# A graph stack on one core: the third hop's weights folded into the first hop's, its sums turned by VectorE or by TensorE

## Chip, cores and metric

The kernel runs on one core of a Trainium2 chip. The time is device microseconds of one execution; the median of three runs before the change is 708.03 us (707.58 to 708.05). One more execution was recorded by the hardware profiler, and all lines quoted are from that one.

The engines carry their names as the profile writes them: PE is TensorE (PEld its weight loads), DVE VectorE, ACT ScalarE, POOL GpSimd, SP SyncE, which issues the loads of the adjacency.

## What is computed

A stack of four small graph networks over one graph of 3327 nodes with 64 features, all in fp32, each with a layer norm and a relu ahead of it and a residual around it. The change concerns the third, whose weight matrix is the adjacency squared element by element (`left_weights` and `A` are both `adj`):

```python
def _L2_gnn_ref(x, A, left_weights, W0, b0, W1, b1, W2, b2):
    w = left_weights * A
    for W, b in ((W0, b0), (W1, b1), (W2, b2)):
        x = w @ x
        x = x @ W.T + b
    return x
...
    # --- layer 2 (adj_preln) ---
    h = jnp.maximum(_layernorm(x, axis=-1), 0.0)
    x = x + _L2_gnn_ref(h, adj, adj, L2_gnn_W0, L2_gnn_b0, L2_gnn_W1, L2_gnn_b1, L2_gnn_W2, L2_gnn_b2)
```

No function that isn't linear stands between the three hops, so a weight on the right of one hop can be applied on the right of an earlier one. A bias that is added before a hop has to pass that hop too.

## The kernel before

**Tiles.** The 3327 nodes are padded to 26 blocks of 128, in two halves of 13. A tile of the adjacency holds 128 source nodes (its partitions) against the destination nodes of a group, for both halves. The 13 destination blocks of a half form four chunks, 0 to 3, of 384, 384, 384 and 512 columns; chunks 0 and 1 are group 0, chunks 2 and 3 group 1. One unit of work (`propagate`, L579) multiplies one tile into the sums of one chunk: two matmuls, one for each half, into the upper and lower 64 partitions of a PSUM bank, so that the sums come out as features by nodes (64 features of each half on 128 partitions). The sources of the next hop are wanted as nodes by features, so each hop's sums are turned around once.

**Hops.** There are eight, k = 0 to 7. 0 and 1 belong to a gated cell, 2 is a ranked sum, 3 to 5 are the three hops of the third network, with squared adjacency, and 6 and 7 belong to the last one. `after_k` (L938 to L1021) is what happens to a chunk whose sums of hop k are complete; `y[k+1]` holds its result for the next hop.

**Order.** The adjacency is read from HBM again and again, since the 20 slots (`slots`, L120) hold less than half of it. `joint(g, k, sweep, later, keep)` (L655) lets a tile serve two hops while it is there: hop k for both chunks of a group, and hop k + 1 of the same group `later` tiles afterwards. So joint(1, 4) runs hops 4 and 5 of group 1, then joint(0, 5) runs hops 5 and 6 of group 0, then joint(1, 6). The first tiles of joint(0, 5) are those whose sources lie in group 1: hop 6 wants `y[6]` of chunk 2 first, after `later` + 1 tiles of hop 5.

All this is written into a list of units at build time; `run` (L711) walks through it and issues the instructions of each engine in that order. What `after_k` does is a generator that yields an estimated number of microseconds; `spend` (L374) counts them down as units pass, so the steps of such a task are strewn among the units. Each engine then runs its own list strictly as written, with semaphores between engines.

**Squares.** A unit of hops 3 to 5 needs its tile squared. In joint(1, 2), (0, 3) and (1, 4) that is done in place once for each chunk; in joint(0, 5) the squares go into other rooms, halves of a slot (`Mask`, L419), since hop 6 wants the plain tile. Squares are issued some units ahead (`expand`, L484, up to 3; `prepare`, L444, up to 6). Who does them is decided at build time, by whether any task of a chunk is open:

```python
    def square(sq, v, turn):
        if turn % 3 or any(ch in tasks or (2, ch) in sums for ch in range(NC)):
            nc.scalar.activation(sq, v, AF.Square)
        else:
            nc.vector.tensor_tensor(sq, v, v, ALU.mult)
```

**PSUM.** There are eight banks, four named `sum` and four named `temp`; `take` and `give` (L316, L329) pass them around by age.

**Weights of the third network.** `bd` (L123) holds four block-diagonal 128x128 matrices: 0 the weight of the second network, 1 to 3 W0, W1 and W2, transposed. `brow` has the biases b0, b1, b2 spread over all partitions, `hopcol` has columns of biases. `product(i, j)` (L205) replaces `bd[i]` by `bd[i]` times `bd[j]`: a pair of matmuls turns `bd[i]`, ScalarE copies, a second pair multiplies, ScalarE copies back. `fold_hops` (L219), which runs once, around 223 to 231 us, multiplies W0 by W1 in this way and passes b0 through W1. Then:

- after_3 (L973) copies the sums, multiplies by `bd[1]` on TensorE, which also turns them, and adds `brow[0]`.
- after_4 (L985) has no weight left to apply: `sums_to_nodes` (L807) copies the sums on ScalarE with the bias column b1 and lets VectorE turn them, in 16 transposes of 32x32 blocks for a chunk.
- after_5 (L988) copies the sums (VectorE for even chunks, ScalarE for odd ones), multiplies by `bd[3]`, W2, on TensorE (`dense_to_nodes`, L759), adds the result from PSUM to x (`residual`, L852), normalizes for hop 6, and at the end turns `y[6]` to features on VectorE (`transpose_on_vector`, L796), which after_6 reads much later.
- b2 is added to x long before, at the end of after_2 (L961), 15 estimated microseconds after the rest of that task, by `add_row` (L859).

Of the kernel before, what the change touches and what calls it, by code (L numbers as in the profile page):

```python
# [9 lines left out]
F32 = mybir.dt.float32  # L10
BF16 = mybir.dt.bfloat16
I16 = mybir.dt.int16
AF = mybir.ActivationFunctionType
ALU = mybir.AluOpType
# [30 lines left out]
N, D = 3327, 64  # L45
P = 128
# [8 lines left out]
CWM = 512  # L55
GROUPS = [(0, 1), (2, 3)]
# [9 lines left out]
WL1, WL2, WL3 = 14, 15, 18  # L66
# [21 lines left out]
def sources_of(*chunks):  # L88
    return [s * NB + b for c in chunks for s in range(2) for b in range(*CH[c])]


def upper(n):
    return slice(n * D, (n + 1) * D)
# [3 lines left out]
def kernel(  # L97
# [9 lines left out]
    nc = tc.nc  # L107
# [3 lines left out]
    work = ctx.enter_context(tc.tile_pool(name="work", bufs=4))  # L111
# [11 lines left out]
    bd = const.tile([P, 4, P], F32, name="bd")  # L123
# [8 lines left out]
    hopcol = const.tile([P, 2], F32, name="hopcol")  # L132
    ident = const.tile([P, P], F32, name="ident")
# [71 lines left out]
    def product(i, j):  # L205

        n, ps = take()
        mm(ps[:, :P], bd[:, i, :], ident)
        tr = work.tile([P, P], F32, name="t2")
        nc.scalar.copy(tr, ps[:, :P])  # L210
        give(n)
        yield 1.0
        n, ps = take()
        mm(ps[:, :P], tr, bd[:, j, :])
        nc.scalar.copy(bd[:, i, :], ps[:, :P])
        give(n)
        yield 1.0

    def fold_hops():  # L219

        i, ps = take()
        for n in range(3):
            for h in range(2):
                nc.tensor.matmul(ps[upper(h), n * P:(n + 1) * P], brow[:, n], ident, start=True, stop=True)
        cols = work.tile([P, CWM], F32, name="t2")
        nc.scalar.copy(cols[:, :3 * P], ps[:, :3 * P])
        give(i)
        yield 1.0

        i, ps = take()  # L230
        mm(ps[:, :D], cols[:, :P], bd[:, 2, :D])
        nc.vector.tensor_copy(brow[:, 0], ps[:, :D])
        nc.vector.tensor_copy(hopcol[:, 0:1], cols[:, P:P + 1])
        give(i)
        yield 1.0
        yield from product(1, 2)
# [59 lines left out]
    def blocks(c):  # L296
        return CH[c][1] - CH[c][0]

    def width(c):
        return blocks(c) * P  # L300

    def mm(out, lhsT, rhs, start=True, stop=True):


        for h in range(2):
            hs = slice(h * D, (h + 1) * D)
            nc.tensor.matmul(out[hs], lhsT[:, hs], rhs, start=start, stop=stop)  # L307
# [8 lines left out]
    def take(sums=False, either=True):  # L316


        either = either and not sums
        pool = idle_sums if sums else idle_temps  # L320
        if either and idle_sums and (not pool or released[idle_sums[0]] < released[pool[0]]):
            pool = idle_sums
        for c in list(tasks):
            if not pool and c not in running:
                advance(c)
        i = pool.popleft()
        return i, banks[i]

    def give(i):  # L329
        released[i] = max(released) + 1  # L330
        (idle_sums if i < 4 else idle_temps).append(i)

    def nodes(c):

        return feat.tile([P, blocks(c), 2, D], F32, name=f"y{c}")

    def flat(t):
        return t.rearrange("p b s d -> p b (s d)")
# [4 lines left out]
    def xchunk(c):  # L343
        return xs[:, CH[c][0]:CH[c][1]]

    def view(ps, c):
        return ps[:, :width(c)].rearrange("p (b f) -> p b f", f=P)
# [5 lines left out]
    def advance(c):  # L353
        running.add(c)
        try:
            tasks[c][1] = next(tasks[c][0])
        except StopIteration:
            del tasks[c]
        running.discard(c)
# [257 lines left out]
    def put(k, c, t):  # L617
        units.append((k, c, t))
        if k == COUNT or KIND[k] != RANKED or c == GROUPS[t.g][0]:
            t.uses += 1  # L620
# [34 lines left out]
    def joint(g, k, sweep, later, keep, lag=None):  # L655


        a, b = GROUPS[g]
        in_place = KIND[k] != PLAIN and KIND[k + 1] == SQUARED
        early = (KIND[k], KIND[k + 1]) == (PLAIN, RANKED)  # L660
        waiting = deque()
        counting = Counting(g, lag)

        def both(t):
            for c in (a, b):
                put(k, c, t)
            if lag is not None:
                counting.add(t)

        def second(n):  # L670
            for _ in range(n):
                if waiting:
                    t = waiting.popleft()
                    for c in (a, b):
                        put(k + 1, c, t)

        for q in sources_of(*GROUPS[1 - g]):
            t = Tile(q, g, in_place, early)
            both(t)
            waiting.append(t)  # L680
            if len(waiting) > later:
                second(1)
        own = [[Tile(q, g, in_place, early) for q in sources_of(c)] for c in (a, b)]
        all_own = own[0] + own[1]
        for n, t in enumerate(all_own[:-sweep]):
            both(t)
            second(len(waiting) + n + 1 > later if early else min(2, len(waiting) - keep))
        counting.rest()
        for c in (a, b):
            for t in all_own[-sweep:]:  # L690
                put(k, c, t)
                if lag is not None and c == a:
                    counting.add(t)
            if KIND[k] == RANKED:
                units.append((k, c, SPECIAL))
        counting.rest()
        second(len(waiting))
        for t in own[0]:
            for c in (a, b):
                put(k + 1, c, t)  # L700
        for c in (a, b):
            for t in own[1]:
                put(k + 1, c, t)
            if KIND[k + 1] == RANKED:
                units.append((k + 1, c, SPECIAL))
# [44 lines left out]
    def evacuate(acc, c, busy=False):  # L750
        m = work.tile([P, CWM], F32, name="t2")[:, :width(c)]
        if c % 2 or busy:
            nc.scalar.copy(m, acc[0][1][:, :width(c)])
        else:
            nc.vector.tensor_copy(m, acc[0][1][:, :width(c)])  # L755
        give(acc[0][0])
        return m

    def dense_to_nodes(ft, w, c):  # L759

        i, ps = take()
        v = view(ps, c)
        for b in range(blocks(c)):
            mm(v[:, b, :], ft[:, b * P:(b + 1) * P], bd[:, w - WL1, :])
        return i, v
# [41 lines left out]
    def sums_to_nodes(acc, c, bias):  # L807

        m = work.tile([P, CWM], F32, name="t2")[:, :width(c)]
        nc.scalar.activation(m, acc[0][1][:, :width(c)], AF.Identity, bias=hopcol[:, bias:bias + 1])  # L810
        give(acc[0][0])
        yield 0.8
        v = m.rearrange("p (b q n) -> p b q n", q=4, n=32)
        yk = nodes(c)
        for s in range(2):
            for f in range(2):
                at = s * D + f * 32
                for q in range(4):
                    nc.vector.transpose(yk[q * 32:(q + 1) * 32, :, s, f * 32:(f + 1) * 32], v[at:at + 32, :, q])  # L819
                yield 1.2  # L820
        return yk
# [30 lines left out]
    def residual(v, c, relu=False):  # L852
        if relu:
            nc.vector.scalar_tensor_tensor(flat(xchunk(c)), v[1], 0.0, flat(xchunk(c)), op0=ALU.max, op1=ALU.add)
        else:
            nc.vector.tensor_tensor(flat(xchunk(c)), flat(xchunk(c)), v[1], ALU.add)
        give(v[0])

    def add_row(c, i):  # L859

        n = 2 * blocks(c)
        nc.vector.tensor_tensor(groups(xchunk(c)), groups(xchunk(c)),
                                brow[:, i:i + 1, :].to_broadcast([P, n, D]), ALU.add)
# [97 lines left out]
    def after_2(c, acc):  # L961
        m = evacuate(acc, c)
        yield 1.4
        v = dense_to_nodes(m, WL1, c)
        yield 1.2
        residual(v, c)
        yk = nodes(c)
        yield from layernorm_relu(yk, c, squares_on_scalar=c in GROUPS[0])
        y[3][c] = yk
        yield 15.0  # L970
        add_row(c, 2)

    def after_3(c, acc):  # L973
        m = evacuate(acc, c)
# [11 lines left out]
        y[5][c] = yield from sums_to_nodes(acc, c, 0)  # L986

    def after_5(c, acc):  # L988
        m = evacuate(acc, c)
        yield 0.8  # L990
        v = dense_to_nodes(m, WL2 + 2, c)
        yield 0.8
        residual(v, c)
        yk = nodes(c)
        yield from layernorm_relu(yk, c)
        y[6][c] = yk
        yield 8.0
        yield from transpose_on_vector(yk, c)
# [30 lines left out]
    joint(1, 2, sweep=6, later=6, keep=1)  # L1029
    joint(0, 3, sweep=8, later=4, keep=4)  # L1030
    joint(1, 4, sweep=8, later=4, keep=4)
    joint(0, 5, sweep=8, later=4, keep=4)
    joint(1, 6, sweep=8, later=4, keep=4)
    alone(0, 7, sweep=6, parts=True)

# [50 lines left out]
```

## Time and profile before

| what | value |
|---|---|
| median of three runs | 708.03 us |
| profiled execution, its time | 707.41 us |
| profiled execution, its span | 705.5 us |
| mean granted TensorE clock | 0.999 |
| TensorE busy | 680.6 us |
| VectorE, ScalarE busy | 351.7, 271.3 us |
| third network's hops 3 to 5 | within some 285 to 561 us |
| matmuls of the units in fp32 (L607) | 3016 records, 533.6 us |
| end of hop 5 for group 1, group 0 | near 512, near 560 us |

The span runs from the first to the last instruction. A matmul in fp32 leaves two records, so a unit is four records of L607. A line of the timeline gives the start, the length, the engine, the line of the kernel, what was written from what, the shape, how many instructions were merged, and in brackets how long the engine had been idle and what released it. In the chain of waits each line is a start, a length, an engine and what ran.

### The profile page before, as it was taken

What the parts mean: (1) busy time and instruction counts of PE and PEld (TensorE: products, weight loads), DVE (VectorE), ACT (ScalarE), POOL (GpSimd) and SP (SyncE); (2) the same over time, 40 slices, a digit from 0 to 9 for tenths busy, and PEclk for the clock granted to TensorE, in tenths of its full rate; (3) what the DMA queues carried; (4) which work ended last, traced back from release to release, by engine and by line L of the source; (5) the groups of instructions that cost most, each with busy time, mean ns of one, the idle gap of its engine ahead of it and who ended that gap; (6) DMA issues with size and microseconds to landing.
All of it is one profiled execution on the core that took longest, in us unless ns stands there. A gap on an engine that the chain in (4) does not pass through costs nothing.

```text
span 705.5 us, 12624 instructions
## 1 busy us (share of the span) xinstructions
PE 680.6 (96%) x5100; PEld 362.5 (51%) x5100; DVE 351.7 (50%) x747; ACT 271.3 (38%) x421; POOL 75.7 (11%) x114
## 2 busy tenths in 40 slices
PE   1999999999999999999999999999999999999997
PEld 1454666643545787677444444333344444344464
DVE  7566835633997889847533105425271565005101
ACT  1014100212136888888997206832166500000101
POOL 4300000002291233111100000000000000000000
PEclk9999999999999999999999999999999999999999
DMA  9999996089688952683799649963997399917991
GB/s 337 401 387 404 405 406 239 1 337 384 204 284 299 313 176 83 241 296 103 266 369 354 242 163 408 405 262 112 392 366 271 105 397 405 407 64 282 403 402 36
DMA packets 68549, 201.31 MB, mean 285 GB/s; under 512 B 7228, under 2 KB 8228, under 8 KB 68492
## 3 DMA queue, kind: packets, MB, share of 16 engines
q1 hardware_dynamic: 65596, 199.46, 76.1%
q8 instruction: 40, 0.66, 0.4%
q10 hardware_dynamic: 720, 0.85, 0.3%
q0 software_dynamic: 2176, 0.20, 0.2%
q14 instruction: 17, 0.14, 0.1%
HBM read 199.45 MB, written 0.85 MB: 284 GB/s over the span
## 4 chain that ended last, share of the span: by engine, by line
PE 84%; DVE 9%; ACT 4%; issue 1%; DMA 1%; SPq 0%; ACTq 0%; DVEq 0%
PE sum L607 70%; PE temp L307 5%; ACT adj L440 4%; DVE adj L466 3%; PE temp L542 2%; PE temp L876 2%; PE sum L307 1%; PE temp L774 1%; PE sum L876 1%; DVE e L521 1%; DMA bd<-in_weights 1%; DVE both L825 1%; DVE adj L901 1%; DVE st L842 0%; DVE t L836 0%
## 5 line engine op out<-in xcount | busy, mean ns | idle before, releaser
L607 PE MATMUL sum<-adj,y 128*64 128x384 f32 (+3 forms) x3016 | 533.6, 501 | 0.8 <-DVE y L849 0.6
L607 PEld LDWEIGHTS sum<-adj,y 128*64 128x64 f32 x3016 | 233.7, 137 | 246.3 <-issue 220.9
L440 ACT ACTIVATE adj<-adj 128x768 f32<-128x768 f32 (+1 forms) x175 | 143.6, 892 | 47.3 <-PE sum L607 24.6
L466 DVE TENSOR_SCALAR adj<-adj 128x768 bf16<-128x768 f32 (+3 forms) x208 | 114.7, 599 | 39.1 <-PE temp L542 31.1
L824 ACT COPY both<-sum 64x384 f32<-64x384 f32 (+3 forms) x17 | 8.1, 478 | 196.4 <-PE sum L607 196.3
L607 PE MATMUL sum<-e,both 128*64 128x384 bf16 (+1 forms) x624 | 78.4, 339 | 0.5 <-DVE e L521 0.4
L523 ACT ACTIVATE e<-temp,bitsb 128x384 int16<-128x384 f32 (+1 forms) x117 | 66.1, 606 | 15.0 <-PE temp L307 9.9
L825 DVE COPY both<-sum 64x384 f32<-64x384 f32 (+3 forms) x17 | 9.7, 568 | 113.6 <-ACT both L824 112.4
L442 DVE TENSOR_TENSOR adj<-adj 128x768 f32<-128x768 f32 (+1 forms) x33 | 31.5, 1003 | 52.2 <-DMA adj<-in_adjT 33.4
L307 PE MATMUL temp<-adj,tri 128*64 128x384 bf16 (+1 forms) x332 | 56.8, 341 | 0.5 <-DVE e L521 0.2
L845 POOL TENSOR_TENSOR st<-st,mhalf 128x6 f32<-128x6 f32 (+1 forms) x16 | 24.5, 1529 | 288.9 <-DVE st L843 288.9
L607 PEld LDWEIGHTS <-both 128*64 128x64 bf16 x624 | 46.5, 110 | 15.5 <-issue 2.2
L307 PEld LDWEIGHTS <-tri 128*64 128x64 bf16 x416 | 33.4, 110 | 15.3 <-issue 7.4
L521 DVE TENSOR_SCALAR e<-temp 128x384 int16<-128x384 f32 (+1 forms) x49 | 30.1, 617 | 21.1 <-ACT e L523 10.5
L471 POOL DMA_DIRECT2D adj<-totals x52 | 32.7, 630 | 51.5 <-PE temp L307 42.9
L803 DVE STREAM_TRANSPOSE both<-y 32x96 f32<-32x96 f32 (+1 forms) x128 | 35.6, 278 | 2.9
L542 PE MATMUL temp<-adj,behind 128*64 128x384 bf16 x208 | 30.3, 339 | 0.9 <-DVE adj L466 0.7
L819 DVE STREAM_TRANSPOSE y<-t 32x96 f32<-32x96 f32 (+1 forms) x64 | 17.8, 278 | 25.2 <-ACT t L810 24.3
L542 PEld LDWEIGHTS <-behind 128*64 128x64 bf16 x208 | 17.0, 110 | 17.6 <-issue 15.9
L755 DVE COPY t<-sum 128x384 f32<-128x384 f32 x6 | 3.3, 554 | 35.4 <-PE sum L607 35.4
L876 PE MATMUL temp<-both,cells 128*64 128x384 f32 (+1 forms) x68 | 17.7, 521 | 0.2 <-DVE both L825 0.2
L523 ACT ACTIVATE e<-sum,bitsb 128x384 int16<-128x384 f32 (+1 forms) x28 | 16.6, 599 | 2.5 <-PE sum L307 2.0
(132 smaller groups left out, 307.5 us busy)
## 6 DMA issues: line engine op xcount, KB each, us to landing
adj<-in_adjT SPq DMA_DIRECT2D x130, 768.0 KB, 8.5
adj<-in_adjT SPq DMA_DIRECT2D x104, 896.0 KB, 12.5
xs<-in_x SPq DMA_DIRECT2D x1, 640.0 KB
adj<-totals POOLq DMA_DIRECT2D x26, 3.0 KB, 5.3
adj<-totals POOLq DMA_DIRECT2D x26, 3.5 KB, 3.6
out<-xs ACTq DMA_DIRECT2D x2, 192.0 KB
out<-xs ACTq DMA_DIRECT2D x1, 256.0 KB
stage<-in_weights SPq DMA_DIRECT2D x2, 112.0 KB, 13.4
```

The lines of the kernel that those rows point to most:

```text
L307: nc.tensor.matmul(out[hs], lhsT[:, hs], rhs, start=start, stop=stop)
L440: nc.scalar.activation(sq, v, AF.Square)
L442: nc.vector.tensor_tensor(sq, v, v, ALU.mult)
L466: nc.vector.tensor_scalar(t.mask.view[:rows, half], t.view()[:rows, half], 0.0, None, op0=ALU.not_equal)
L471: nc.gpsimd.dma_start(out=t.mask.view[P - 1:P], in_=totals[t.g][t.q:t.q + D + 1:D, :])
L521: nc.vector.tensor_scalar(wide[:, s], ps[:, :w], BITS, 0.0, op0=ALU.add, op1=ALU.max)
L523: nc.scalar.activation(wide[:, s], ps[:, :w], AF.Relu, bias=bitsb)
L542: nc.tensor.matmul(counts[c][1][s * D:(s + 1) * D, :w], behind[:, NQ - 1 - t.q:NQ - 1 - t.q + D], t.mask.view[:, s, t.cols(c)], start=firs ...
L607: nc.tensor.matmul(acc[h][1][h * D:(h + 1) * D, :w], yq[h], rhs[h], start=first and n == 0, stop=last and n == len(terms) - 1)
L803: nc.vector.transpose(to[at:at + 32, :, q], h[q * 32:(q + 1) * 32, :, s, f * 32:(f + 1) * 32])
L845: nc.gpsimd.tensor_tensor(st[:, 3, :n], st[:, 2, :n], mhalf[:, :n], ALU.pow)
L876: nc.tensor.matmul(ps[upper(1 - s), :w], cells[:, cell, s, g, :], both[c][:, s], start=True, stop=True)
```

## The change

W2 is folded too. `fold_hops` first multiplies W1 by W2 (`product(2, 3)`), so that b0 passes W1 and W2 and, later, W0 is multiplied by both; b1 is passed through W2 by one more pair of small matmuls, and b2 is kept as a second column of `hopcol`. after_3 and after_4 are as before, with other contents of `bd[1]`, `brow[0]` and `hopcol`. In after_5 no weight is left:

- for group 1, `sums_to_nodes` copies the sums on ScalarE with b2 and turns them in 16 transposes of VectorE, and one add joins them to x;
- for group 0, ScalarE copies the sums with b2, and TensorE turns them by multiplying with the identity, in the same number of matmuls as it multiplied by W2 before.

The add of b2 at the end of after_2 goes, and with it the 15 microseconds for which that task stayed open. joint(0, 5) gets `later=6` in place of 4.

```diff
@@ fold_hops
+        yield from product(2, 3)
         i, ps = take()
         mm(ps[:, :D], cols[:, :P], bd[:, 2, :D])
+        mm(ps[:, D:2 * D], bd[:, 3, :], cols[:, P:P + D])
         nc.vector.tensor_copy(brow[:, 0], ps[:, :D])
-        nc.vector.tensor_copy(hopcol[:, 0:1], cols[:, P:P + 1])
+        nc.vector.tensor_copy(hopcol[:, 0:1], ps[:, D:D + 1])
+        nc.vector.tensor_copy(hopcol[:, 1:2], cols[:, 2 * P:2 * P + 1])
         give(i)
         yield 1.0
         yield from product(1, 2)
@@ after_2
         y[3][c] = yk
-        yield 15.0
-        add_row(c, 2)
@@ after_5
-        m = evacuate(acc, c)
-        yield 0.8
-        v = dense_to_nodes(m, WL2 + 2, c)
-        yield 0.8
-        residual(v, c)
-        yk = nodes(c)
+        if c in GROUPS[1]:
+            yk = yield from sums_to_nodes(acc, c, 1)
+            nc.vector.tensor_tensor(flat(xchunk(c)), flat(xchunk(c)), flat(yk), ALU.add)
+        else:
+            m = work.tile([P, CWM], F32, name="t2")[:, :width(c)]
+            nc.scalar.activation(m, acc[0][1][:, :width(c)], AF.Identity, bias=hopcol[:, 1:2])
+            give(acc[0][0])
+            yield 1.0
+            i, ps = take()
+            v = view(ps, c)
+            for b in range(blocks(c)):
+                mm(v[:, b, :], m[:, b * P:(b + 1) * P], ident)
+            yield 1.0
+            residual((i, v), c)
+            yk = nodes(c)
         yield from layernorm_relu(yk, c)
@@ schedule
-    joint(0, 5, sweep=8, later=4, keep=4)
+    joint(0, 5, sweep=8, later=6, keep=4)
```

Some facts of the built instruction order are used below. After the change group 1's transposes stand on VectorE before the adds to x; four of chunk 3's stand among the steps of chunk 2's normalization. The first squares of joint(0, 5) stand on ScalarE as before: three, then the copy of chunk 3, then the rest, eleven of them in a row of seven tiles. Five squares of hop 3 in chunks 2 and 3 move from ScalarE to VectorE, by the rule in `square`. The loads on SP stand in the same order, in other slots.

## The prediction

> **What bounds the kernel now.** I read the page's busy shares first, then its chain of waits in order of time, then the timelines of ScalarE and VectorE around the end of the third hop, then a table of stretches of 5 us.
>
> ```profile
> PE 680.6 (96%) x5100; PEld 362.5 (51%) x5100; DVE 351.7 (50%) x747; ACT 271.3 (38%) x421; POOL 75.7 (11%) x114
> ...
> PE 84%; DVE 9%; ACT 4%; issue 1%; DMA 1%; SPq 0%; ACTq 0%; DVEq 0%
> ```
>
> TensorE is the bound, and the chain that sets the end runs 84% through it. So a matmul that is taken away counts in full wherever TensorE goes straight on, and work on VectorE or ScalarE counts only where TensorE waits for it. The chain (start, length, engine and line, count) shows that for the stage that is changed:
>
> ```profile
> 355.19 8.47 ACT adj L440 x10
> ...
> 365.16 1.09 PE temp L307 x16
> 366.25 41.28 PE sum L607 x256
> ...
> 414.00 91.51 PE sum L607 x508
> 506.19 7.30 PE sum L607 x36
> 513.49 0.87 PE temp L307 x16
> 514.36 41.28 PE sum L607 x256
> ```
>
> See two holes in the stream of L607. From 414.00 + 91.51 = 505.51 to 506.19 stand 0.68 us for chunk 2's multiplication by W2, and at 513.49 stand 0.87 us for chunk 3's. Before and after them the stream keeps 41.28/64 = 0.645 us for a unit of 384 columns (four records) and waits for nothing. ScalarE's timeline after the second hole:
>
> ```profile
> 507.13 2.31 ACT L440 ACTIVATE adj<-adj 128x768 f32<-128x768 f32 x3 [21.93 <-PE sum L607]
> 512.29 0.59 ACT L753 COPY t<-sum 128x512 f32<-128x512 f32 x1 [2.85 <-issue]
> 512.77 5.38 ACT L440 ACTIVATE adj<-adj 128x768 f32<-128x768 f32 x7
> 518.97 1.58 ACT L440 ACTIVATE adj<-adj 128x768 f32<-128x768 f32 x2 [0.82 <-ACT adj L440]
> ```
>
> L440 squares the adjacency for each unit of hop 5. Three squares run early, the fourth stands behind chunk 3's copy, and from there they come every (5.38 - 0.83)/6 = 0.76 us (0.83 is the length of one), slower than TensorE's 0.645. VectorE helps with none of them there, since `square` gives all to ScalarE while a task is open. The table of stretches, for where the weights are folded (PE, PEld, DVE, ACT, POOL busy, clock, DMA):
>
> ```profile
> 225.00:230.00 5.00, 4.74 (x79) 3.99 (x77) 4.24 (x10) 3.81 (x9) 0.00 (x0) 1.00 0.93 320
> 230.00:235.00 5.00, 4.88 (x74) 3.72 (x71) 4.83 (x10) 3.18 (x7) 0.00 (x0) 1.00 0.93 310
> 235.00:240.00 5.00, 3.94 (x44) 2.84 (x42) 4.79 (x13) 4.25 (x9) 1.71 (x2) 1.00 1.03 392
> ```
>
> Here TensorE is idle for 0.26 + 0.12 + 1.06 = 1.44 us, and VectorE is nearly full: VectorE sets the pace.
>
> **What the Trainium skill says.** "VectorE: DVE Perf Modes", The three transpose paths: VectorE transposes only blocks of 32x32, TensorE a whole 128x128. The trace agrees in kind: hop 4's change of layout (L819) takes 16 instructions for a chunk, each of 32 partitions, 271 ns for 96 columns and 308 ns for 128. "TensorE: Matmul & The Clock Gate", its table of figures: ScalarE and VectorE take their queues in strict order. The trace agrees: chunk 3's copy at 364.54 stands behind squares that run without a gap, although its last sum was done near 363.6. "Perfetto Trace Analysis", Tensor Engine Instruction: the end of a matmul in a profile is computed, not observed; so I take differences of starts on the chain, not busy time.
>
> **The change part by part.**
>
> *Group 1's multiplication goes (after_5, chunks 2 and 3).* The 12 and 16 records of L307 leave the chain: -0.68 - 0.87 = -1.55 us. From the timeline of weight loads one can read 1.40 to 1.66, by where a unit is taken to begin.
>
> *In its place: two activations and 32 transposes.* Chunk 2's sum is ready at 504.70. Activation 0.58 (L810), 16 x 0.271 = 4.34, residual 0.56, the first three instructions of the normalization 0.55 + 0.17 + 0.56: 511.5. In the built order four transposes of chunk 3 come next, whose source is ready at 511.52 + 0.58 = 512.1 (its sum ends where TensorE begins group 0, at 513.49 - 2 x 0.645 = 512.20, now 0.68 earlier). Then 4 x 0.308 = 1.23, square, reduce and scale 1.28, 12 x 0.308 = 3.70, last instruction 0.56: y[6] of chunk 2 near 519.1, against 511.63 now. Hop 6 first asks for it after 7 tiles, 14 units: 511.52 + 9.03 = 520.6. So 1.5 us are left, more if TensorE itself is late (next part). With the old `later=4` it would be asked for at 511.52 + 10 x 0.645 = 518.0, and TensorE would wait 1.1 us; that is what the seven tiles cover. Chunk 3's y[6] comes near 525.5 and is asked for after 536. Behind these instructions on VectorE stand only the transposes to features that hop 6's end needs, until now done at 529.4, then near 535, and squares from 542. Cost 0; if the cover is gone, one for one.
>
> *Seven tiles of hop 5 in a row in place of five.* Count from the start of group 0's hop 5 (0). ScalarE's copy of chunk 3 starts at 0.09 and the fourth square at 0.57, as now. Square k (k from 4) is done at 0.57 + 0.76 (k - 4) + 0.83, and unit k wants it at 0.645 (k - 1). For unit 10, the last in a row now, that is 5.96 against 5.81, covered by the hole of 0.87. The hole is gone, and the row ends with unit 14: 9.00 against 8.39. So TensorE is late by 0.61, with a signal's way some 0.65. Bounds: 0.3 (squares every 0.735, as the runs of four have it) and 1.1 (a weight load, which comes some 0.3 to 0.5 before its matmul, carries the wait). After that hop 6 gives 1.29 us for each tile, and ScalarE catches up. Taken: +0.65. The DMA is not late: the tiles of this row were issued by 499.58; the last tile of this group is now asked for at 538.95, then near 542 (its slot is a room for squares until then), and is used after 552.
>
> *Folding W2 in.* `product(2, 3)` adds two pairs of 128-column matmuls (0.22 us a pair on the chain at 229.71) and one of 64 columns (some 0.15): 0.59 us of TensorE, two ScalarE copies of 0.26, and one VectorE copy of 0.14; three small VectorE copies move some 5 us down its queue, from a place where it then waited 0.25 for TensorE to one where it runs without a gap. TensorE's part fits into the 1.44 us; VectorE's 0.4 (0.22 + 0.14 + 0.14 less overlap) doesn't. Taken +0.4; bounds 0 (VectorE idles later) and 0.9 (both parts in full).
>
> *b2 moves.* Four adds leave VectorE (3 x 0.55, 0.68). They stood at 289 to 297, 341.51 and 358.11, where TensorE waits for none of them: 0. For group 0 `ident` takes the place of W2 with the same number of matmuls: 0. Chunk 0's sum is copied by ScalarE behind one more square: 554.7 + 0.58 = 555.3, in time for TensorE at 555.64. Five later squares of that sweep move back by 0.58 and one more joins them; by the same count each is still 0.5 us before its matmul: 0, at worst 0.3.
>
> *A side effect.* The add held a task open for 15 us. Without it, `square` gives five of hop 3's squares of chunks 2 and 3 to VectorE, idle from 348.47 to 356.10 (some 3 x 0.96 + 2 x 1.28 = 5.4 us, the wider one an estimate by width). ScalarE is 4 us less loaded before 364.54, chunk 3's copy no longer stands behind squares, and TensorE's wait of 0.27 before 365.16 goes: -0.27, at least 0.
>
> Sum: -1.55 + 0.65 + 0.4 - 0.27 = -0.77 us. The profiled execution took 707.41 (span 705.5 and 1.9 around it), so 706.6 for it. The median of the runs is 708.03, 0.6 above it; the same step gives 707.3.
>
> **Rivals.**
>
> *The full gain.* ScalarE keeps up, as it does through unit 10 now, and VectorE's idle moments swallow the fold: -1.55 - 0.27 = -1.8, 706.2. For it: both costs are sums of small margins. Against: 0.76 over 0.645 is a rate, not an accident.
>
> *The fold stage slips.* Slower: between 225 and 250 the banks of PSUM turn in another order, and TensorE and VectorE take turns there. One such wait is 0.91 us (before 236.05). If three more appear, +2.7 in place of 0.4: -0.77 + 2.3 = +1.5, 709.6. It decides from 2.2 us more idle TensorE there. For it: ScalarE's last copy of the fold stands behind a 1.04 us activation. Against: from 240 on TensorE waits 0.3 at most at a time.
>
> *y[6] of chunk 2 is late.* If the chain of 14 us above runs 4 us longer, hop 6 waits 1.9 (1.5 and the 0.65 of lateness cover the rest): -0.77 + 1.9 = +1.1, 709.1; from 4.3 us longer on it is slower by over 0.2%. For it: all of it is one queue. Against: each step has a measured duration.
>
> **How the numbers follow.** Chances: forecast 0.50, full gain 0.27, fold stage 0.13, late y[6] 0.10. The measurement can tell about 0.2%, 1.4 us, from no change. The forecast's own range is -1.66 - 0.27 + 0.3 = -1.6 to -1.40 + 1.1 + 0.9 + 0.3 = +0.9: 706.4 to 708.9, nearly all within 0.2%. The full gain is faster. The fold stage is slower; late y[6] is half slower, half the same, and the forecast's upper edge and what I haven't seen add 0.04. That makes faster 0.26, same 0.52, slower 0.22. The range takes in the full gain's 706.2 with the runs' own 0.25 either way, and the slower cases up to 709.6: 705.8 to 709.6.
>
> **What would show it.** In the profile after: the stream of L607's successor runs through from 505 to 513 with no L307 in it; ScalarE squares without a gap over some 10 us after chunk 3's copy, and the units at the end of that row stand 0.76 apart; hop 6's first unit waits for a square, not for the normalization; TensorE's idle time from 225 to 240 stays under 2 us; no wait before the multiplication near 365. Wrong would be: a wait for y at hop 6, a second wait of 0.9 us near 236, or a wait for a tile from HBM after 540.

## The result, and the profile after

The changed kernel takes 706.89 us (median of 17 runs, 705.45 to 707.72) beside 708.05 for the kernel before (17 runs, 707.33 to 708.88): ratio 0.9984, interval 0.9977 to 0.9990. That is 1.2 us less (0.7 to 1.6), where 0.8 were predicted (707.3). The profiled execution took 706.55 with a span of 704.8.

The chain of waits after the change, in order of time (start, length, engine and line, count). The lines have moved by three: L610 is L607 of before, L310 L307, L443 L440.

```profile
221.86 0.97 PE temp L879 x6
...
266.54 0.97 PE sum L610 x12
...
329.08 0.81 PE sum L610 x10
...
358.17 7.30 PE sum L610 x36
365.47 0.87 PE temp L310 x16
366.35 41.28 PE sum L610 x256
...
414.09 140.78 PE sum L610 x800
554.87 0.66 PE temp L310 x12
555.53 5.16 PE sum L610 x32
```

See that the stream is unbroken from 414.09 to 554.87: both holes of before, 0.68 and 0.87, are gone. Before, the same 800 records took 91.51 + 7.30 + 41.28 = 140.09 us, now 140.78, so the stream itself became 0.69 longer. These lines also give marks by which every kernel of this study can be measured in three stages; the last mark is the line of 32 records after group 0's first multiplication.

| stage | before | after |
|---|---|---|
| fold: from the first line of 0.97 shown to the second (before: 221.58 to 265.98) | 44.40 | 44.68 |
| hop 3: to the 41.28 us line (before: 328.50 to 366.25) | 37.75 | 37.27 |
| end of hop 5: to the 5.16 us line (before: 366.25 to 556.30) | 190.05 | 189.18 |

The differences, +0.28, -0.48 and -0.87, sum to -1.07. The stretches between and after them are as they were: 62.54 us from 266.54 to 329.08 (62.52 before) and 149.27 after the last mark (149.20 before). What stands before the first mark differs between executions by up to some 2 us whatever the kernel (220.72 to 222.85 over all kernels here), so the marks tell more than the spans do.

The 0.69 can't be seen in TensorE's busy time: its row shows no gap there. The timeline of its weight loads shows it (idle time in brackets, with what released it):

```profile
512.42 0.14 PEld L610 LDWEIGHTS sum<-adj,y 128*64 128x64 f32 x2 [0.18 <-ACT t L813]
...
519.73 0.20 PEld L610 LDWEIGHTS sum<-adj,y 128*64 128x64 f32 x4 [0.54 <-ACT adj L443]
520.46 0.20 PEld L610 LDWEIGHTS sum<-adj,y 128*64 128x64 f32 x4 [0.54 <-ACT adj L443]
520.84 0.14 PEld L610 LDWEIGHTS sum<-adj,y 128*64 128x64 f32 x2 [0.18 <-DVE st L837]
```

From 513.14 to 520.46 the units stand 0.73 us apart, each released by a square of ScalarE (L443), where 0.645 is TensorE's own pace. ScalarE squares without a gap meanwhile:

```profile
512.25 8.16 ACT L443 ACTIVATE adj<-adj 128x768 f32<-128x768 f32 x11
```

At 520.84 hop 6 begins, with no more idle time than any load has (the view names L837, a later instruction of VectorE, but 0.18 us is what loads have that wait for nothing). VectorE's timeline shows that its source was there:

```profile
515.05 3.78 DVE L822 STREAM_TRANSPOSE y<-t 32x128 f32<-32x128 f32 x12
518.87 0.56 DVE L852 SCALAR_TENSOR_TENSOR y<-t,st 128x384 f32<-128x384 f32 x1
```

The last line completes `y[6]` of chunk 2 at 519.43, 1.4 us ahead of 520.84.

### The profile page after: what moved, and what is told of

It is laid out like the page before. It is cut to its first block, busy times and chain, and to the rows that moved or that the text cites. A ratio compares the mean times of both kernels' runs of the same rounds, so it can differ in the third digit from the quotient of the medians.

```text
span 704.8 us, 12628 instructions
## 1 busy us (share of the span) xinstructions
PE 680.4 (97%) x5084; PEld 362.3 (51%) x5084; DVE 361.7 (51%) x779; ACT 268.8 (38%) x420; POOL 80.2 (11%) x114
## 4 chain that ended last, share of the span: by engine, by line
PE 91%; DVE 7%; issue 1%; ACT 0%; DMA 0%; POOL 0%; ACTq 0%; DVEq 0%; POOLq 0%
PE sum L610 77%; PE temp L310 5%; PE temp L545 2%; PE temp L879 2%; PE sum L310 1%; PE temp L777 1%; DVE adj L469 1%; PE sum L879 1%; DVE e L524 1%; DVE adj L904 1%; DVE st L845 1%; DVE st L837 1%; DVE t L839 1%; DVE y L844 0%; DVE both L828 0%
## 5 line engine op out<-in xcount | busy, mean ns | idle before, releaser
L610 PE MATMUL sum<-adj,y 128*64 128x384 f32 (+3 forms) x3016 | 534.9, 503 | 0.6 <-DVE y L852 0.6
L610 PEld LDWEIGHTS sum<-adj,y 128*64 128x64 f32 x3016 | 233.6, 137 | 248.8 <-issue 219.2
L443 ACT ACTIVATE adj<-adj 128x768 f32<-128x768 f32 (+1 forms) x170 | 139.3, 891 | 27.8 <-DMA adj<-in_adjT 13.9
L610 PE MATMUL sum<-e,both 128*64 128x384 bf16 (+1 forms) x624 | 78.5, 339 | 0.5 <-DVE e L524 0.5
L828 DVE COPY both<-sum 64x384 f32<-64x384 f32 (+3 forms) x17 | 9.7, 568 | 114.0 <-ACT both L827 112.8
L526 ACT ACTIVATE e<-temp,bitsb 128x384 int16<-128x384 f32 (+1 forms) x108 | 60.8, 606 | 12.9 <-PE temp L310 8.7
L445 DVE TENSOR_TENSOR adj<-adj 128x768 f32<-128x768 f32 (+1 forms) x38 | 36.4, 1010 | 47.6 <-DMA adj<-in_adjT 34.7
L310 PE MATMUL temp<-adj,tri 128*64 128x384 bf16 (+1 forms) x332 | 56.7, 341 | 0.6 <-DVE e L524 0.6
L610 PEld LDWEIGHTS <-both 128*64 128x64 bf16 x624 | 46.7, 110 | 15.4 <-issue 2.3
L822 DVE STREAM_TRANSPOSE y<-t 32x96 f32<-32x96 f32 (+1 forms) x96 | 26.9, 281 | 40.5 <-ACT t L813 39.2
L524 DVE TENSOR_SCALAR e<-temp 128x384 int16<-128x384 f32 (+1 forms) x58 | 34.9, 607 | 22.7 <-ACT e L526 10.9
L310 PEld LDWEIGHTS <-tri 128*64 128x64 bf16 x416 | 33.4, 110 | 13.4 <-issue 5.2
L806 DVE STREAM_TRANSPOSE both<-y 32x96 f32<-32x96 f32 (+1 forms) x128 | 35.6, 278 | 2.9
L526 ACT ACTIVATE e<-sum,bitsb 128x384 int16<-128x384 f32 (+1 forms) x37 | 21.8, 602 | 5.5 <-PE sum L310 3.9
L813 ACT ACTIVATE t<-sum,hopcol 128x384 f32<-128x384 f32 (+1 forms) x6 | 3.7, 614 | 48.8 <-PE sum L610 48.8
L567 POOL MEMSET adj<- 128x768 f32 (+1 forms) x2 | 1.9, 952 | 146.0 <-PE sum L610 146.0
```

Source lines behind the costliest of these rows:

```text
L524: nc.vector.tensor_scalar(wide[:, s], ps[:, :w], BITS, 0.0, op0=ALU.add, op1=ALU.max)
L526: nc.scalar.activation(wide[:, s], ps[:, :w], AF.Relu, bias=bitsb)
L610: nc.tensor.matmul(acc[h][1][h * D:(h + 1) * D, :w], yq[h], rhs[h], start=first and n == 0, stop=last and n == len(terms) - 1)
L806: nc.vector.transpose(to[at:at + 32, :, q], h[q * 32:(q + 1) * 32, :, s, f * 32:(f + 1) * 32])
```

## The experiments

Ten kernels ran. The table has their three stages by the marks above, and the ratio to the kernel before, each with its interval; medians within some 0.5 us of each other are not told apart by the runs, while stages that should be equal repeat to 0.03. A dash stands where the chain of a kernel has no such line.

| kernel | fold | hop 3 | end of hop 5 | median | ratio to before |
|---|---|---|---|---|---|
| later4 | 44.66 | 37.27 | 190.12 | 707.93 | 0.9997 (0.9989 to 1.0005) |
| before_later6 | 44.41 | 37.75 | 190.05 | 707.75 | 0.9996 (0.9989 to 1.0004) |
| pool_squares | 44.66 | - | 188.58 | 705.40 | 0.9966 (0.9954 to 0.9978) |
| one_vector_square | 44.66 | 37.26 | 188.57 | 706.29 | 0.9975 (0.9969 to 0.9982) |
| before_fold | 44.66 | 37.75 | 190.05 | 708.26 | 1.0004 (0.9996 to 1.0013) |
| before_no_hold | 44.42 | 37.26 | 190.05 | 708.51 | 1.0008 (1.0000 to 1.0016) |
| identity_all | 44.65 | 37.26 | 190.03 | 707.57 | 0.9992 (0.9984 to 1.0000) |
| vector_all | 44.66 | 37.26 | - | 712.72 | 1.0063 (1.0050 to 1.0077) |
| fold_on_scalar | 44.40 | 37.26 | 189.18 | 706.19 | 0.9979 (0.9970 to 0.9989) |
| best | 44.40 | 37.26 | 188.57 | 705.52 | 0.9969 (0.9958 to 0.9981) |

### Is the row of seven tiles needed, and what does it cost?

**later4**, from the changed kernel:

```diff
-    joint(0, 5, sweep=8, later=6, keep=4)
+    joint(0, 5, sweep=8, later=4, keep=4)
```

> The changed kernel with joint(0, 5) back at later=4: five tiles of hop 5 in a row, not seven. My theory (VectorE's chain to chunk 2's y[6] needs the longer row): the row ends some 2.6 us earlier, near 518, while y[6] of chunk 2 is complete at 519.4 in the changed kernel's trace, so hop 6's first unit waits for VectorE by about 1.0 to 1.3 us; the shorter row gives back some 0.35 us of lateness behind the squares; in sum 0.6 to 1.0 us slower than the changed kernel, and a wait for VectorE's L852 appears near 518. Rival (the longer row is not needed, and only costs): no such wait, and up to 0.4 us faster than the changed kernel.

Measured: 190.12 us, and a median of 707.93. TensorE's timeline:

```profile
520.42 9.90 PE L610 MATMUL sum<-adj,y 128*64 128x384 f32 x60 [1.08 <-DVE y L852]
```

Now there is a gap of 1.08 us, released by the last instruction of the normalization, L852. With five tiles in a row the whole gain of the stage is lost, as the prediction's 1.1 us for this case had it.

**before_later6** does the opposite, `later=6` in the kernel before.

> The kernel before with later=6 alone. My theory (what the longer row costs is ScalarE's pace of 0.73 us a square against TensorE's 0.645 us a unit, and the hole of 0.87 us for chunk 3's multiplication hides it): within 0.3 us of the kernel before over the stretch from 500 to 530 us, units near 0.65 apart for most of the row. Rival (the longer row costs something by itself, such as later loads): 0.7 us or more slower over that stretch, or TensorE waits for a tile after 540.

Measured: 190.05, as before. There the hole of 0.87 still stands at the row's start and lets ScalarE get ahead. So the longer row by itself costs nothing; it costs 0.69 only together with the hole's absence.

### Is it ScalarE's rate that takes 0.69 back?

Two kernels relieve ScalarE of a part of that row, from the changed kernel. **pool_squares** gives three squares to GpSimd:

```diff
-            square(wide, t.view(c), t.q + c)
+            if c == GROUPS[0][0] and t.q in (8, 20, 9):
+                nc.gpsimd.tensor_tensor(wide, t.view(c), t.view(c), ALU.mult)
+            else:
+                square(wide, t.view(c), t.q + c)
```

> The changed kernel with three of the squares of the row of seven tiles (chunk 0, third, fifth and seventh tile) given to GpSimd, which is idle there. My theory (ScalarE's squares pace the row): ScalarE has three squares fewer, 2.2 us against a lateness of 0.9, so TensorE's units stand 0.645 apart and the stretch from 512 to 523 is 0.6 to 0.9 us shorter than in the changed kernel, if one square takes GpSimd under some 2.5 us and VectorE's chain isn't slowed. Rival (TensorE itself is slower in the row, or the time is lost on the way to y[6]): no change, or later by what GpSimd's slow square adds.

**one_vector_square** gives a single one to VectorE, into a moment in which it waits:

```diff
-            square(wide, t.view(c), t.q + c)
+            if c == GROUPS[0][1] and t.q == 7:
+                nc.vector.tensor_tensor(wide, t.view(c), t.view(c), ALU.mult)
+            else:
+                square(wide, t.view(c), t.q + c)
```

> The changed kernel with one square of the row (chunk 1, second tile) given to VectorE. My theory: ScalarE has 0.73 us less to do, so the row's lateness of 0.9 shrinks to 0.2; but VectorE's chain to chunk 2's y[6] grows by 0.5 to 0.95 us, to 519.9 to 520.4, about when hop 6 asks for it; in sum 0.3 to 0.7 us shorter than the changed kernel over 505 to 525. Rival (the row isn't paced by ScalarE): no shorter, or longer by up to 0.9 us.

Measured: 188.58 and 188.57, 0.60 and 0.61 us less than the changed kernel. The weight loads of one_vector_square (its L613 is L610 of the changed kernel):

```profile
516.37 0.14 PEld L613 LDWEIGHTS sum<-adj,y 128*64 128x64 f32 x2 [0.18 <-issue]
516.77 0.39 PEld L613 LDWEIGHTS sum<-adj,y 128*64 128x64 f32 x4 [0.26 <-ACT adj L443]
...
518.97 0.20 PEld L613 LDWEIGHTS sum<-adj,y 128*64 128x64 f32 x4 [0.52 <-ACT adj L443]
```

One square less gives ScalarE a lead of 0.73 us, and only the last four units are paced by it. VectorE's chain to `y[6]` of chunk 2 grew by less than expected, by 0.29 us (complete at 518.83, which is 153.37 after the mark near 366, against 519.43 and 153.08), since 0.48 us of the square fell into a wait for chunk 3's copy. So the squares' rate is shown to be the cause: taking away one of them on another engine gives nearly all of the 0.69 back. In pool_squares one square of GpSimd takes 1.47 us, and three units wait for one; by this stage it does not do better. Its median, 705.40 from five runs, is the lowest of the table, but its interval and that of one_vector_square overlap between 0.9969 and 0.9978, and no stage of its profile is shorter: from the mark near 266 to the one near 366 it takes 100.05 us, where the changed kernel takes 99.81. Why that stretch is longer stays open.

### What does the fold cost, and why?

**before_fold** adds the fold's work to the kernel before; nobody reads what it makes. `product` gets a third argument, the tile to write.

```diff
+    spare23 = const.tile([P, P], F32, name="spare23")
...
+        yield from product(2, 3, spare23)
         i, ps = take()
         mm(ps[:, :D], cols[:, :P], bd[:, 2, :D])
+        mm(ps[:, D:2 * D], bd[:, 3, :], cols[:, P:P + D])
         nc.vector.tensor_copy(brow[:, 0], ps[:, :D])
+        nc.vector.tensor_copy(hopcol[:, 1:2], ps[:, D:D + 1])
         nc.vector.tensor_copy(hopcol[:, 0:1], cols[:, P:P + 1])
```

> The kernel before, with the fold of W2 added as extra work whose results nobody reads: product(2, 3) into a spare tile, one more 64-column matmul and one more small VectorE copy. My theory: in the VectorE-paced stage TensorE's part fits in its idle time and some of VectorE's part shows, so from the chain's marker near 221 to the one near 266 the time is 44.40 + 0.27 = 44.7 us (44.4 to 45.0), as in the changed kernel (44.68), and the median is 0.1 to 0.5 us above the kernel before. Rival, TensorE pays in full: 44.40 + 0.59 = 45.0 or more. Rival, the 0.27 is only the early offset of 0.28 still being absorbed and the fold is free: 44.4.

Measured: 44.66 against 44.40, with the other stages as before. So the fold alone costs 0.26, and the +0.28 of the changed kernel is no drift. Of the median (+0.25 us, interval -0.3 to +0.9) no more can be said than that it doesn't contradict. Where the fold's copies stand on VectorE in the changed kernel:

```profile
232.53 0.56 DVE L839 TENSOR_TENSOR t<-xs,st 128x384 f32<-128x384 f32 x1
233.01 0.22 DVE L234 COPY brow<-temp 128x64 f32<-128x64 f32 x1
233.14 0.15 DVE L235 COPY hopcol<-temp 128x1 f32<-128x1 f32 x1
233.21 0.14 DVE L236 COPY hopcol<-t 128x1 f32<-128x1 f32 x1
233.27 0.55 DVE L524 TENSOR_SCALAR e<-temp 128x384 int16<-128x384 f32 x1
```

From the first copy's start to the start of L524 pass 233.27 - 233.01 = 0.26 us. **fold_on_scalar** puts these three copies of the changed kernel on ScalarE:

```diff
-        nc.vector.tensor_copy(brow[:, 0], ps[:, :D])
-        nc.vector.tensor_copy(hopcol[:, 0:1], ps[:, D:D + 1])
-        nc.vector.tensor_copy(hopcol[:, 1:2], cols[:, 2 * P:2 * P + 1])
+        nc.scalar.copy(brow[:, 0], ps[:, :D])
+        nc.scalar.copy(hopcol[:, 0:1], ps[:, D:D + 1])
+        nc.scalar.copy(hopcol[:, 1:2], cols[:, 2 * P:2 * P + 1])
```

> The changed kernel, with the three small copies of the fold (64 columns, and two single columns) on ScalarE instead of VectorE. My theory: what the fold costs is VectorE's part, since VectorE sets the pace there, so from the marker near 221 to the one near 266 the time falls below the 44.68 us of the changed kernel, by some 0.27 to 0.5 us, to 44.2 to 44.4. Rival, the fold's cost is TensorE's and ScalarE's chain of products: 44.68 or more.

Measured: 44.40, to the hundredth what it was without the fold. VectorE's queue in it:

```profile
231.59 0.56 DVE L839 TENSOR_TENSOR t<-xs,st 128x384 f32<-128x384 f32 x1
232.07 0.55 DVE L524 TENSOR_SCALAR e<-temp 128x384 int16<-128x384 f32 x1
```

L839 to L524 now takes 0.48 in place of 0.74. The added matmuls and the two copies of `product(2, 3)` on ScalarE are still there and cost nothing that the marks show. VectorE's three small copies are the whole price. Two of the three stand in the kernel before too, but some 5 us earlier, from 227.01 to 227.28, just ahead of a wait of VectorE for TensorE: from 226.54 to 227.53 VectorE took 0.99 us with them, and takes as long without them after the change (226.83 to 227.82).

### Does closing the task early bring the gain in hop 3?

**before_no_hold**, from the kernel before:

```diff
-        yield 15.0
         add_row(c, 2)
```

> The kernel before, with b2 added at once instead of 15 estimated us later; nothing else is changed. My theory: the task closes early, five squares of hop 3 go to VectorE, ScalarE reaches chunk 3's copy in time, and the stretch from the marker near 329 to the end of the multiplication near 366 takes 37.75 - 0.48 = 37.27 us, with no wait ahead of the multiplication; the median falls by some 0.5 us. Rival, the gain there came from the fold or from chance: 37.75 us and no change of the median.

Measured: 37.26, so the stage is confirmed to 0.01; the median is not: 708.51, 0.5 us above before and not below. TensorE's timeline around the multiplication, in the kernel before and then here:

```profile
357.41 7.47 PE L607 MATMUL sum<-adj,y 128*64 128x512 f32 x36
365.16 1.09 PE L307 MATMUL temp<-bd,t 128*64 128x128 f32 x16 [0.27 <-ACT t L753]
366.08 2.11 PE L607 MATMUL sum<-adj,y 128*64 128x384 f32 x12
```

```profile
358.52 7.47 PE L607 MATMUL sum<-adj,y 128*64 128x512 f32 x36
365.82 1.04 PE L307 MATMUL temp<-bd,t 128*64 128x128 f32 x16
366.69 1.78 PE L607 MATMUL sum<-adj,y 128*64 128x384 f32 x10
```

The wait ahead of the multiplication is gone. From the start of the 36 records to that of the multiplication pass 7.75 us before and 7.30 here, and from there to the next start 0.92 and 0.87: 0.50 in all (0.49 by the marks), 0.45 of it the wait. The bracket shows only 0.27 of that wait, since it counts from the computed end of the 36 records, and this end lies 0.17 us (7.47 - 7.30) after the next start where TensorE goes straight on. The loss lies earlier, and my expectation overlooked it: done at once, two of the four adds fall on VectorE where it still sets the pace.

```profile
282.86 0.55 DVE L862 TENSOR_TENSOR xs<-xs,brow 128x384 f32<-128x384 f32 x1
283.33 0.55 DVE L521 TENSOR_SCALAR e<-temp 128x384 int16<-128x384 f32 x1
```

This is the second of the two; the first starts at 274.41 and what follows it at 274.88. Each takes 0.47 from its start to the next start, 0.94 together. From the mark near 266 to the first chain line of 1.83 us there (12 records near 285) pass 286.31 - 266.14 = 20.17 us against 285.20 - 265.98 = 19.22 before: +0.95. So the delay of 15 us had a use in the kernel before: it kept two adds out of this stretch, at the price of five squares on the wrong engine later. The change drops the adds altogether and has neither cost.

### Which part of the change earns the end of hop 5?

**identity_all** keeps W2 folded and `later=6`, but lets TensorE turn group 1 as well:

```diff
-        if c in GROUPS[1]:
+        if c not in range(NC):
             yk = yield from sums_to_nodes(acc, c, 1)
```

> The changed kernel, with group 1's sums too turned by TensorE with the identity instead of by VectorE; W2 stays folded, later stays 6. My theory: what the change wins in this stage is only the two multiplications taken off TensorE less the row paced by ScalarE's squares, so both holes of 0.68 and 0.87 come back and the row's lateness goes: 189.18 + 0.87 = 190.05 us from the marker near 366 to the last chain line of the squared hops near 555, as in the kernel before, and the median is 0.8 to 0.9 us above the changed kernel, 707.8. Rival, the gain came from later=6 or from b2 on ScalarE: 189.2 us and no loss.

Measured: 190.03, and a median of 707.57. The holes are back and the row is no longer late. So in this stage only VectorE's turning of group 1 counts, and neither b2 in ScalarE's copy nor the longer row gains anything.

**vector_all** goes the other way and lets VectorE turn group 0 too:

```diff
-        if c in GROUPS[1]:
+        if c in range(NC):
             yk = yield from sums_to_nodes(acc, c, 1)
```

> The changed kernel, with group 0's sums too turned by VectorE. My theory, which takes the choice by group for right: two more multiplications of 0.66 and 0.65 us leave TensorE (-1.31), but chunk 0's and 1's y[6] come some 4.5 us later than now against a margin of 2 to 2.7 us, so TensorE waits for a VectorE instruction near 565 and 573, 1 to 3 us in all; the net is 0 to 2 us slower than the changed kernel, 707 to 709. Rival, the margin holds: -1.3 us, 705.6, and no wait on VectorE there.

Measured: 712.72, some 5.8 us above the changed kernel; the direction was expected, the size was missed by far. TensorE's timeline:

```profile
568.24 7.96 PE L610 MATMUL sum<-adj,y 128*64 128x384 f32 x48 [3.25 <-DVE y L852]
578.20 5.38 PE L610 MATMUL sum<-adj,y 128*64 128x384 f32 x32 [2.00 <-DVE y L852]
```

Two waits for the end of a normalization, 5.25 us by this view. To the chain's line of 42.77 us (583.59 after the change, 589.53 here) it is 589.53 - 367.16 = 222.37 against 583.59 - 366.35 = 217.24 us: +5.13. With the 1.31 that TensorE no longer spends on group 0, the delays must sum to 6.4. Distances between starts, at 0.645 us a unit, find them: 3.7 us ahead of 568.24 (31 units from 544.55 on would have ended at 564.55; some 0.3 of it are units that come late before the wait), 2.2 ahead of 578.20 (12 units from 568.24), and 0.5 at a third place, 588.73, where TensorE waits for a copy of VectorE (L828) that stands behind the transposes of L806. VectorE has no idle time from 555.28 to 573:

```profile
555.28 4.51 DVE L822 STREAM_TRANSPOSE y<-t 32x96 f32<-32x96 f32 x16 [1.53 <-ACT t L813]
...
565.34 2.25 DVE L822 STREAM_TRANSPOSE y<-t 32x96 f32<-32x96 f32 x8
567.62 0.56 DVE L852 SCALAR_TENSOR_TENSOR y<-t,st 128x384 f32<-128x384 f32 x1
568.22 4.52 DVE L806 STREAM_TRANSPOSE both<-y 32x96 f32<-32x96 f32 x16
572.75 0.56 DVE L992 TENSOR_TENSOR xs<-xs,y 128x384 f32<-128x384 f32 x1
```

I had counted each chunk's own 16 transposes against its own margin. But chunk 1's 16 (eight from 561.69, eight from 565.34) stand among the steps of chunk 0's normalization, and chunk 0's turning back to features (L806) stands ahead of chunk 1's normalization, so each chunk pays some 4.5 us a second time. For group 1 the same interleaving is there, but with `later=6` hop 6 asks for it only after seven tiles.

### Both mends together

**best** is the changed kernel with the edits of one_vector_square and fold_on_scalar.

> The changed kernel with both mends: one square of the row on VectorE (as in one_vector_square) and the fold's three small copies on ScalarE. My theory: the gains add, since the two stages lie apart: 188.57 us from the marker near 366 to the last chain line of the squared hops, 44.2 to 44.4 us from 221 to 266, a median of 705.9 to 706.2, 0.25 to 0.3% under the kernel before. Rival, the 0.3 us of the fold is taken back in the wait-bound stretch from 266 to 366: 706.3.

Measured: 44.40, 37.26 and 188.57, and a median of 705.52 against 707.76 of the kernel before, measured with it (ratio 0.9969, 0.9958 to 0.9981). The stages add up: 0 - 0.49 - 1.48 = -1.97 us against before. It beats the kernel before. Against the changed kernel its marks are 0.28 and 0.61 us better, but the intervals of the two ratios overlap between 0.9977 and 0.9981, so that it beats the changed kernel too rests on the marks more than on the medians.

## Why the prediction was right

**Group 1's multiplication, -1.55, and the row, +0.65.** Right as two terms: the holes are gone (identity_all brings them back), and the row took 0.69 back, by ScalarE's squares, as one_vector_square shows. In sum -0.86 by the chain's lines where -0.90 was said. What bound the row was named before the run, and seen where it was said to be seen: in the distance between units. One sign was named wrongly: hop 6's first unit was to wait for a square, but only the units of hop 5 ahead of it do. That 0.65 came so near to 0.69 is luck in part. The squares came every (8.16 - 0.83)/10 = 0.733 us and not every 0.76, which by the prediction's own count takes 0.27 off. Against that, the weight load of the last unit was 0.94 us late (520.46, against 512.42 + 11 x 0.645 = 519.52), and the count had left the wait of the loads to its upper bound. Both lie within the bounds that were stated, and they nearly cancel.

**y[6] of chunk 2.** Said 519.1 (the steps as listed sum to 518.9) and asked for at 520.6, or later where TensorE is late; measured 519.43 and 520.84. The row of seven tiles is what makes it hold: with five, the gap was 1.08.

**The fold, +0.4.** Mis-sized: 0.26. The mechanism was right (TensorE's part hidden, VectorE's shown), but I summed the three copies' durations, less a guess of the overlap. What an instruction takes from a full queue is the distance to the next start: 0.26 for the three. The rival that the whole stage would slip did not come; TensorE's idle time from 225 to 240 is 5.00 x 3 - 4.84 - 3.95 - 4.68 = 1.53 us against 1.44, by the table of stretches.

**The side effect, -0.27.** Mis-sized: -0.48. The mechanism was right, but I took the bracket's 0.27 for the whole wait, although I had said that the end of a matmul in the profile is computed. From start to start the wait was 0.45, as the timelines of before_no_hold show. ScalarE's timeline of the changed kernel shows why the wait went: the copy stands behind no square.

```profile
354.53 5.87 ACT L443 ACTIVATE adj<-adj 128x1024 f32<-128x1024 f32 x7
364.23 0.59 ACT L756 COPY t<-sum 128x512 f32<-128x512 f32 x1 [3.83 <-PE sum L610]
```

From 354.53 on seven squares and then 3.83 us of idle time, where before twelve went from 354.25 up to the copy. The remaining 0.04 or 0.05, by which the multiplication itself is shorter from start to start, goes with the wait, in before_no_hold as in the changed kernel; its cause is not shown.

**b2's move, 0.** Right for the place where the adds stood. before_no_hold adds the boundary to it: some 15 us earlier two of them would have cost 0.94.

With the measured sizes the sum is -1.55 + 0.69 + 0.28 - 0.48 = -1.06 where -0.77 was said. Both errors of size were on the same side, and together with the row they make 0.3 of the 0.4 us between 707.3 and 706.89; what is left is less than the medians can tell. The full gain of -1.8 did not come in the changed kernel; best reaches -1.97 by its marks (with -0.48 in hop 3, where that rival had -0.27), since both of that rival's conditions (the row on time, the fold free) had to be made.

## What to carry to other kernels

Where work is taken off the bounding engine, the hole that it left may have been what another engine used to catch up: compare the rates of the two over the stretch after it, and look for the pacing in the distances between units, not in busy time. Take the length of a wait of TensorE from the starts on both sides, not from the idle time in brackets. Price a small instruction in a full queue by the distance between starts, not by its duration. When work moves to an engine with slack, count what other chunks put into the same queue between the steps of the chain; the same edit that gained 0.9 us in one group cost over 5 in the other.

## What was not expected of the hardware

- Two instructions of VectorE were slower beside a square of GpSimd, each seen once: in pool_squares L847 took 0.63 and L855 0.65 us where their like took 0.56, and both overlap one (511.49 to 512.96 and 516.79 to 518.25), while the transposes beside the square between them (514.07 to 515.54) took 3.79 against 3.78. The Trainium skill, "GPSIMD Engine Reference", Specifications, says that GpSimd contends with VectorE's instructions that have two inputs in SBUF; the trace agrees, since L847 and L855 have two and a transpose has one. It costs only some 0.1 us each.
- A square of 128x768 in fp32 has a length of 1.47 us on GpSimd (pool_squares), 0.96 on VectorE (one_vector_square) and 0.83 on ScalarE; to the next start VectorE takes 0.88 there and ScalarE 0.73.
